# A scan stage on one core: the time step by one Softplus from PSUM, and another table of places

## The chip, the cores and the metric

The kernel runs on one core of a Trainium2 chip. The metric is device time in microseconds (us), the median of some runs. The engines are TensorE (PE; its weight loads are shown as PEld), VectorE (DVE), ScalarE (ACT), GpSimd (POOL) and SyncE (SP), which issues all DMAs here. PSUM is where PE writes; SBUF is the working memory.

## The reference

Four layers work in turn on 64 images of 128 channels by 28x28 pixels (784): a quantised convolution block, an attention block, a Mamba block over the 784 pixels (a selective scan), and a second Mamba over eight tokens a pixel with a group norm. The change is in the third layer. What it must compute, cut to the part that matters, for 160 inner channels d and 24 states n:

```python
delta = jax.nn.softplus(dt @ W_dt.T + b_dt)          # 160 x 784 an image, rank 8
A = -jnp.exp(A_log)
h = jnp.exp(d_t[..., None] * A) * h + (d_t * u_t)[..., None] * B_t[:, None, :]
y = jnp.einsum('bdn,bn->bd', h, C_t)
```

softplus(x) is log(1 + exp(x)); h runs over time, the 784 pixels.

## The kernel before, in words

The program has three stages one behind another: the convolutions (L132-229), a joint stage for attention and the first Mamba (attention_and_mamba, L614-1198; "the scan stage" here), and the token Mamba (token_mamba, L1200 on).

In the scan stage four kinds of work overlap over the images. attention (L783) computes queries and keys (qt, kt), the row maxima mx on DVE, the exponentials et on ACT from products qt,kt in a PSUM bank, and the sums et,vt on PE. inputs (L899; its places are called "prepare") makes the inner channels u, the gate z, the rows B and C (sent to DRAM as bcd), and the time step; delta and delta times u go to DRAM as dud, ten DMAs an image. The scan itself takes 30 pieces an image, five groups of 32 channels by six groups of four states, each a tile of 128x784: inject on POOL (h = ur * Br), decay on ACT (a = exp(dr * A), into one of two PSUM buffers, L1106), scan on DVE (tensor_tensor_scan), the product with Cr on DVE for 18 of the pieces and on POOL for 12, and sums on PE (y from h by fold). The rows Br, Cr, dr and ur are spread by DMA from bcd and dud. The tiles h have nine buffers (L1094). after (L1019; "end") projects out and writes the inputs of the token stage (tok). All matmuls outside the two kinds with own PSUM tiles (a, y) share three PSUM banks called bank.

The time step before (L970-989): the low-rank product is read from PSUM twice, by Abs and by Relu (six activations), then by softplus(x) = relu(x) + ln(1 + exp(-|x|)) with a correction of the rounding of 1 + e: Exp, Identity and Ln on ACT, one operation on DVE (ab), two on POOL (pos), and a third on POOL for delta times u. The tiles are 128x980 (784 pixels of the first 128 channels, and 196 columns that hold the other 32 in four quarters), from a rotation of three buffers ("both", L778).

Nobody writes the order of this stage by hand. The Python code only records steps in a Plan (L343), and Plan.order (L510) walks a list scheduler: for each engine it takes, among the steps that are ready, the one of lowest rank that can start within a patience; Plan.cost (L477) gives each step an assumed duration and a lag to the steps behind it. Where a plan has a table of places, the rank is 30 times the image plus the number that SCAN_PLACES (L255) has for that step of an image (L516-518). So the table and the assumed durations together decide what stands in each engine's queue; the engines then work through their queues strictly, waiting on semaphores. The token stage has a Plan of its own without a table (it is built with turns False). All instructions of both plans are issued at L595, so that this line stands on nearly every row of the profile, and the tile names tell them apart.

[...]EXP_LN holds Exp and Ln; silus (L892) loads SILU, runs its group and loads EXP_LN again, for u and z and for tok: four loads an image.

Of the kernel before, what the change touches and what calls it, by code (L numbers as in the profile page):

```python
# [19 lines left out]
AF = mybir.ActivationFunctionType  # L20
ALU = mybir.AluOpType
# [206 lines left out]
class Tables:  # L228
# [20 lines left out]
    def use(self, name):  # L249
# [8 lines left out]
        -27.16, 95.44, -15.63, 37.72, -30.51, 57.03, -18.48, -125.52, -178.15, -206.63, -174.65, -197.18,  # L258
        -140.8, -116.57, -149.57, -145.94, -227.75, -111.36, -231.96, -171.87, -173.54, -260.5, -273.42,
        -234.6, -172.96, 10.23, -238.49, -198.04, -9.89, -98.73, -142.5, -119.15, -169.38, -62.95, -220.79,  # L260
        -175.82, -246.73, -295.07, -241.57, -310.14, -274.17, -171.92, -254.19, -311.49, -254.96, -322.3,
        -304.01, -357.57, -440.14, -292.13, -474.41, -320.29, -299.91, -499.4, -397.94, -447.26, -211.4,
        -457.68, -289.19, -314.57, -355.54, -378.5, -341.25, -386.43, -360.43, -490.97, -420.49, -429.83,
        -423.33, -579.73, -530.76, -409.94, -351.63, -324.83, -200.92, -293.69, -397.03, -369.21, -413.66,
        -326.13, -292.8, -382.29, -530.85, -505.9, -426.91, -268.63, -329.47, -406.22, -284.33, -330.23,
        -329.88, -373.65, -354.09, -591.18, -489.62
    ],
    "prepare": [
        -66.92, -102.03, -163.16, -47.03, -103.5, -28.71, -36.86, -46.92, -14.15, -68.57, -96.79, -43.76,
        -9.97, -14.28, -81.51, -17.75, -143.82, -133.62, -89.23, -86.81, -7.36, -92.05, -46.28, 9.23, -0.72,  # L270
        137.5, 74.4, -3.52, -61.63, 47.04, -140.23, -40.33, 37.88, 10.06, -119.58, -6.08, -114.83, -162.58,
        -81.55, -59.2, -187.99, -199.29, -242.26, -6.88, -148.55, -80.7, -52.51, -83.71, -227.33, -125.92,
        -134.66, -35.74, -156.84, -76.92, -60.72, -100.66, -90.48, -87.39, -83.33, -44.33, -184.83, 8.93,
        -122.37, -16.94, -91.6
    ],
    "inject": [
        18.78, -13.04, 39.46, -108.54, -24.16, 8.2, -12.14, 22.57, 73.89, 71.93, 173.68, 188.48, -7.76,
        96.37, 16.03, 77.21, -45.69, -70.69, 26.78, -37.73, -20.28, -51.28, -20.21, 54.87, 95.56, 97.76,
        -73.06, -111.22, -26.41, -52.72, 125.48, -13.26, -27.35, -58.59, -101.61, -144.4, -4.61, -60.31,
        -88.83, 44.3, -73.66, -55.93, -17.9, -28.45, 42.86, -19.08, -6.71, 0.59, -15.68, 33.03, 26.73, 45.2,  # L280
        -30.02, 43.3, 45.01, 18.88, -5.35, -59.09, -62.2, 3.56, 101.99, 59.89, 50.57, -4.07, -66.46, -33.11,
        -59.04, 56.76, -3.76, 49.95, 46.4, 54.58, 78.09, 56.87, 67.69, 78.94, -16.92, 92.45, 162.12, 67.42,
        -27.26, 43.68, -79.78, -22.7, -178.74, -193.89, -149.11, -173.08, -205.47, -217.02, -101.34, -62.16,
        -7.27, -69.71, -80.65, -168.87, -112.09, -96.03, -258.82, -264.84, -190.08, -122.2, -37.5, -160.28,
        23.29, -40.81, -224.12, -94.95, -66.49, -46.3, -106.86, -75.8, -168.43, -150.66, -26.28, 43.69,
        29.69, -93.59, -101.58, -130.67, -248.79, -133.16, -121.54, -20.97, 35.67, 78.52, 38.63, 70.37,
        82.72, 64.67, -88.86, 29.57, -136.68, 57.59, 7.34, 51.64, -33.33, -104.67
    ],
    "decay": [
        -95.2, -84.44, 139.88, -72.09, -197.03, -36.24, -233.95, 27.53, -70.69, -167.37, -8.97, -131.49,  # L290
        -187.81, -41.37, -86.9, 81.55, -95.01, -242.01, -137.6, -103.85, 116.96, -45.81, -149.11, 40.01,
        65.22, -238.07, -222.67, -41.3, -194.35, -87.31, -260.63, -357.86, 64.48, -220.63, -92.14, -142.66,
        -227.46, -230.49, -195.52, -43.46, -50.78, -15.66, 97.53, -76.33, -111.14, -66.31, 126.12, -4.68,
        29.52, -62.6
    ],
    "scan": [
        64.34, -28.04, -128.29, -88.87, 8.4, -73.1, -3.81, -119.89, -103.54, -114.09, -143.02, -108.94,
        -123.94, -52.99, 129.22, -33.73, 7.38, -59.29, -13.77, -60.97, -181.27, -149.78, -51.55, -55.41,
        -167.42, -266.57, -193.49, -252.04, -122.23, -122.66, -227.09, -92.14, 17.3, -138.99, 5.77, -111.11,
        21.49, -54.75, 140.71, 131.97, 13.77, 6.4, 106.63, -36.26, 10.14, 26.05, 97.46, -26.99, 10.86,  # L300
        -39.78, 63.49, 46.08, 57.9, 41.38, 345.66, 22.26, 49, 94.12, 97.27, -13.26, 88.75, 17.09, -19.63,
        94.73, 147.37, 156.04, 329.27, 79.09, 214.57, 175.56, 123.17, 186.44, 269.79, 249.84, 269.7, 53.44,
        156.54, 11.49, 162.67, 94.54, 92.9, 155.53, 72.47, 66.49
    ],
    "sums": [
        -77.34, -87.75, 6.78, -83.9, -97.13, -138.22, -160.32, -250.84, -177.94, -161.76, -138.4, -245.14,
        -194.82, 68.91, -143.78, -66.16, 16.51, 196.24, -93.37, 233.98, 61.03, 123.4, -10.51, -82.35,
        -139.71, -113.24, -305.16, 238.99, 148.82, 156.94, 279.52, 285.83, 102.28, 101.96, 205.62, 21.76,
        159.55, -38.75, 93.99, -8.89
    ],  # L310
    "end": [
        -152.26, 121.85, 137.04, -40.17, 6.91, 58.09, 7.41, 9.83, -12.72, -154.91, -73.79, 48.34, 5.15,
        6.87, 62.19, -39.12, 29.45, 111.87, 36.96, 15.95, -37.92, 52.34, 70.47, 85.33, 225.7, 147.56,
        -22.61, 43.42, -72.62, 156.66, 47.12, 80.71, 39.11, 91.98, 14.61, 113.76, 79.23, -51.66, 20.25,
        7.12, 127.77, 164.81
# [14 lines left out]
class Step:  # L330


    def __init__(self, engine, at, leading):
        self.engine, self.at, self.leading = engine, at, leading
        self.calls, self.tiles, self.after, self.before = [], [], set(), []
        self.us, self.lag, self.shared = 0.0, 0.07, False


class Plan:
# [95 lines left out]
    def add(self, calls):  # L435
# [9 lines left out]
        for engine, method, args, kw in calls:  # L445
            assert engine == step.engine
            named = list(enumerate(args)) + list(kw.items())
            aps = [(k, a) for k, a in named if hasattr(a, "tensor")]
            outs = [a for k, a in aps if k == 0 or k in self.OUT]
            ins = [a for k, a in aps if not (k == 0 or k in self.OUT)]  # L450
            if method == "matmul" and not kw["start"]:
                reads += [self.span(a)[:3] + (0, 1 << 20) for a in outs]
            writes += map(self.span, outs)
            reads += map(self.span, ins)
            us, shared, lag = self.cost(engine, method, outs, ins, args, kw)
            step.us += us
            step.shared |= shared
            step.lag = lag
        for accesses, wrote in ((reads, False), (writes, True)):
# [17 lines left out]
    def cost(self, engine, method, outs, ins, args, kw):  # L477

# [31 lines left out]
    def order(self, lead, patience):  # L510
# [23 lines left out]
        port = 0.0  # L534
# [19 lines left out]
        while True:  # L554
# [13 lines left out]
            clock[s.engine] = end = at + s.us  # L568
# [10 lines left out]
            for o in s.before:  # L579
                o.ready = max(o.ready, end + (0.0 if o.engine == s.engine and s.engine != "sync" else s.lag))  # L580
                o.open -= 1
                if not o.open:
                    insort(ready[o.engine], o, key=lambda s: s.rank)
# [27 lines left out]
SILU = "silu_and_others"  # L611


def attention_and_mamba(tc, tables, x, c2d, s2, b2x15, x2d, utd, ztd, pk3, pk4, vec, v, ident, eps):  # L614
# [11 lines left out]
    with ExitStack() as ctx:  # L626
# [272 lines left out]
        def inputs(x1):  # L899
# [70 lines left out]
            ab, pos = both("ab"), both("pos")  # L970
            for h in range(2):
                acc = bank()[:, :HT]
                product(acc, [(w("WdtT", 0, C, 8), dt[:, HALF[h]])])
                act(ab[:, h, :HT], acc, AF.Abs, bias=v("bdtA"))
                act(pos[:, h, :HT], acc, AF.Relu, bias=v("bdtA"))
            acc = bank()[:, :QT]
            quarters(acc, [(w("WdtT", C, 160, 8), dt)])
            act(ab[:, :, HT:], eighths(acc), AF.Abs, bias=v("bdtB"))
            act(pos[:, :, HT:], eighths(acc), AF.Relu, bias=v("bdtB"))
            yield  # L980
            act(ab, ab, AF.Exp, scale=-1.0)
            w1 = both("w1")
            act(w1, ab, AF.Identity, bias=1.0)
            plan.vector.scalar_tensor_tensor(ab, w1, 1.0, ab, ALU.subtract, ALU.subtract)
            act(w1, w1, AF.Ln)
            yield
            plan.gpsimd.tensor_tensor(pos, pos, ab, ALU.subtract)
            plan.gpsimd.tensor_tensor(pos, w1, pos, ALU.add)
            plan.gpsimd.tensor_tensor(ab, pos, u, ALU.mult)
            dud = rows_dram.tile([2, 160, T], F32, name="dud")  # L990
            for m, src in enumerate((pos, ab)):
# [640 lines left out]
```

## Time and profile before

| what | value |
|---|---|
| median of 3 runs | 13,503.77 us (13,500.2 to 13,507.47) |
| profiled execution: time, span | 13,484.76 us, 13,482.6 us |
| busy over the span: PE, DVE, ACT, POOL | 10,764.5, 11,302.1, 10,309.6, 10,700.2 us |
| table loads on ACT | 262, of 1283 ns, 336.1 us |
| mean granted clock of TensorE | 0.841 |

In the rows of the profile, a group of instructions is given as line, engine, operation, output<-inputs, shape and count, then its busy time and the mean of one in ns, then the idle time of the engine just before them and whom it waited for. The waits view gives "engine tile line <- engine tile: us in total, times, longest". The timeline has the start in us, the duration in us, then the instruction, and in brackets the idle time before it. A busy time is a union: neighbours on one engine overlap a little, so that the sum of single durations is larger.

### The profile page before, as it was taken

Reading aid. Unit: us, or ns where it says so; the run is one execution under the profiler, and the core shown is the slowest. Engines: PE = TensorE matmul, PEld = TensorE weight load, DVE = VectorE, ACT = ScalarE, POOL = GpSimd, SP = SyncE. Lnnn points to the kernel's source line nnn. Section 1 sums busy time; section 2 is a strip of 40 time slices with the busy share of each in tenths; the row PEclk is TensorE's granted clock in tenths of the full one; section 3 lists DMA queues with packets and bytes.
Section 4 is the critical chain, followed back from the end, with each engine's and each line's share of the span. In section 5 each row is a group of like instructions: output and inputs, shape, how many; then the busy total and the mean of one; then the engine's idle time right before and its main releaser. Section 6 shows DMA issues by size and latency. Waiting matters only on the chain. (4 is left out here: it accounts for less than half of the span.)

```text
span 13482.6 us, 196851 instructions
## 1 busy us (share of the span) xinstructions
PE 10764.5 (80%) x66976; PEld 6721.6 (50%) x66976; DVE 11302.1 (84%) x10312; ACT 10309.6 (76%) x24308; POOL 10700.2 (79%) x5432
## 2 busy tenths in 40 slices
PE   9988888888888888888886677777777777777776
PEld 9644344344434434433433556565555655556554
DVE  3558888888888888888887899999999899999988
ACT  2357777777777777777776888888888888888886
POOL 0048888888888888888887888888888888888887
PEclk9978888888888888888887888888888888888887
DMA  3525544544544554454444111121111111111111
GB/s 130 191 83 144 148 138 143 150 134 141 146 142 136 143 151 134 141 153 137 133 142 132 40 50 58 46 59 45 53 53 48 56 51 54 49 57 51 48 54 44
DMA packets 758799, 1350.57 MB, mean 100 GB/s; under 512 B 212768, under 2 KB 396448, under 8 KB 757792
## 3 DMA queue, kind: packets, MB, share of 16 engines
q1 hardware_dynamic: 757792, 1337.99, 33.9%
q8 instruction: 529, 8.67, 0.3%
q14 instruction: 478, 3.92, 0.1%
HBM read 980.75 MB, written 356.65 MB: 99 GB/s over the span
## 5 line engine op out<-in xcount | busy, mean ns | idle before, releaser
L595 ACT ACTIVATE a<-delta,A 128x98 f32<-128x98 f32 x14336 | 3906.2, 365 | 773.0 <-PE y L595 438.2
L595 POOL TENSOR_TENSOR h<-ur,Br 128x784 f32<-128x784 f32 x1920 | 3566.3, 1885 | 262.5 <-PE y L595 170.0
L595 POOL TENSOR_TENSOR db<-u,BC 128x896 f32<-128x896 f32 x1568 | 3257.0, 2101 | 153.0 <-DVE h L595 145.8
L595 PE MATMUL y<-a,ident 128*128 128x280 f32 x7168 | 2059.7, 452 | 735.3 <-DVE a L595 724.1
L595 DVE TENSOR_TENSOR_SCAN a<-a,h 128x784 f32<-128x784 f32 x1152 | 2048.4, 1783 | 306.5 <-ACT a L595 304.8
L595 ACT ACTIVATE a<-dr,A 128x784 f32<-128x784 f32 x1920 | 1731.6, 914 | 602.8 <-DVE h L595 576.5
L595 PEld LDWEIGHTS y<-a,ident 128*128 128x128 f32 x7168 | 1556.6, 220 | 1241.2 <-issue 416.2
L595 POOL TENSOR_TENSOR h<-h,Cr 128x784 f32<-128x784 f32 x768 | 1431.9, 1872 | 607.2 <-DVE h L595 495.5
L595 DVE TENSOR_TENSOR_SCAN h<-a,h 128x784 f32<-128x784 f32 x768 | 1367.3, 1780 | 260.3 <-ACT a L595 249.8
L595 DVE TENSOR_TENSOR h<-h,a 128x896 f32<-128x896 f32 x1344 | 1476.4, 1098 | 42.5
L595 PE MATMUL y<-h,fold 128*32 128x196 f32 x15360 | 1033.0, 382 | 459.5 <-POOL h L595 362.6
L595 DVE TENSOR_TENSOR h<-h,db 128x896 f32<-128x896 f32 x1120 | 1230.6, 1099 | 87.8 <-POOL db L595 1.9
L595 DVE TENSOR_TENSOR h<-a,Cr 128x784 f32<-128x784 f32 x1152 | 1109.9, 968 | 192.3 <-DMA Cr<-bcd 150.7
L595 PEld LDWEIGHTS y<-h,fold 128*32 128x32 f32 x15360 | 427.3, 119 | 1166.6 <-POOL h L595 554.0
L595 DVE TENSOR_TENSOR a<-h,BC 128x896 f32<-128x896 f32 x896 | 976.7, 1090 | 28.4
L595 PE MATMUL bank<-et,vt 112*128 112x392 f32 x1792 | 963.8, 667 | 1.5 <-ACT et L595 1.4
L595 PEld LDWEIGHTS y<-late,ident 128*128 128x128 f32 x7168 | 834.5, 192 | 19.8 <-issue 0.5
L595 PE MATMUL y<-late,ident 128*128 128x112 f32 x7168 | 834.0, 274 | 0.0
L595 ACT ACTIVATE et<-bank 112x392 f32<-112x392 f32 x896 | 406.3, 490 | 479.7 <-PE bank L595 470.4
L595 POOL TENSOR_TENSOR xn<-s,sq 128x784 f32<-128x784 f32 x64 | 118.7, 1854 | 741.4 <-DVE mx L595 734.3
L595 POOL TENSOR_TENSOR a<-a,db 128x896 f32<-128x896 f32 x224 | 517.3, 2309 | 232.6 <-issue 168.7
L595 PE MATMUL bank<-qt,kt 17*112 17x392 f32 x1792 | 671.5, 704 | 16.2 <-ACT et L595 6.2
(223 smaller groups left out, 19738.1 us busy)
## 6 DMA issues: line engine op xcount, KB each, us to landing
Br<-bcd SPq DMA_DIRECT2D x1536, 98.0 KB
Cr<-bcd SPq DMA_DIRECT2D x1536, 98.0 KB
dr<-dud SPq DMA_DIRECT2D x1280, 98.0 KB
ur<-dud SPq DMA_DIRECT2D x1280, 98.0 KB
utd<-tok SPq DMA_DIRECT2D x128, 392.0 KB
ztd<-tok SPq DMA_DIRECT2D x128, 392.0 KB
rows<-utd SPq DMA_DIRECT2D x192, 256.0 KB
xt<-in_x SPq DMA_DIRECT2D x32, 784.0 KB
```

Of the source, the lines that this page charges most:

```text
L595: last = getattr(getattr(nc, engine), method)(*args, **kw)
```

## The change

The time step now comes from ScalarE's Softplus, read once from PSUM. Two banks are filled, each with half of the 784 pixels (392 columns) of 128 channels, and 98 columns that hold the other 32 channels; the last 32 channels take eight matmuls of 98 columns where they took four of 196. ACT loads the table set SOFTPLUS, runs four activations (392 and 98 elements, twice), and loads EXP_LN again; the planner keeps these six instructions together. DVE's operation and two of POOL's are gone, and delta times u stays. Two buffers of "both" are used an image in place of three.

```diff
-            ab, pos = both("ab"), both("pos")
-            for h in range(2):
-                acc = bank()[:, :HT]
-                product(acc, [(w("WdtT", 0, C, 8), dt[:, HALF[h]])])
-                act(ab[:, h, :HT], acc, AF.Abs, bias=v("bdtA"))
-                act(pos[:, h, :HT], acc, AF.Relu, bias=v("bdtA"))
-            acc = bank()[:, :QT]
-            quarters(acc, [(w("WdtT", C, 160, 8), dt)])
-            act(ab[:, :, HT:], eighths(acc), AF.Abs, bias=v("bdtB"))
-            act(pos[:, :, HT:], eighths(acc), AF.Relu, bias=v("bdtB"))
-            yield
-            act(ab, ab, AF.Exp, scale=-1.0)
-            w1 = both("w1")
-            act(w1, ab, AF.Identity, bias=1.0)
-            plan.vector.scalar_tensor_tensor(ab, w1, 1.0, ab, ALU.subtract, ALU.subtract)
-            act(w1, w1, AF.Ln)
-            yield
-            plan.gpsimd.tensor_tensor(pos, pos, ab, ALU.subtract)
-            plan.gpsimd.tensor_tensor(pos, w1, pos, ALU.add)
-            plan.gpsimd.tensor_tensor(ab, pos, u, ALU.mult)
+            delta, du = both("delta"), both("du")
+            accs = [bank()[:, :HW2] for h in range(2)]
+            for h, acc in enumerate(accs):
+                with plan.claiming(delta, *accs), plan.together():
+                    plan.tensor.matmul(
+                        acc[:, :HT], lhsT=w("WdtT", 0, C, 8), rhs=dt[:, HALF[h]], start=True, stop=False,
+                        skip_group_check=True,
+                    )
+                    for j in range(4):
+                        at = j * QT + h * ET
+                        plan.tensor.matmul(
+                            acc[32 * j : 32 * j + 32, HT:], lhsT=w("WdtT", C, 160, 8), rhs=dt[:, at : at + ET],
+                            start=False, stop=True, skip_group_check=True,
+                        )
+            with plan.together():
+                plan.scalar.preload_act_table_set(SOFTPLUS)
+                for h, acc in enumerate(accs):
+                    act(delta[:, h, :HT], acc[:, :HT], AF.Softplus, bias=v("bdtA"))
+                    act(delta[:, h, HT:], acc[:, HT:], AF.Softplus, bias=v("bdtB"))
+                plan.scalar.preload_act_table_set(EXP_LN)
+            yield
+            plan.gpsimd.tensor_tensor(du, delta, u, ALU.mult)
```

All of SCAN_PLACES is replaced by other numbers, and Plan.cost has other assumed durations for the scan stage (the old function stays as rough, and the token stage keeps it):

```diff
     def cost(self, engine, method, outs, ins, args, kw):
+        if not self.turns:
+            return self.rough(engine, method, outs, ins, args, kw)
...
+        if engine == "sync":
+            return 0.45, False, 4.5
+        if engine == "tensor":
+            us = max(0.115, n / 1030) * 2
+            if outs[0].partition_size() == 32:
+                return us / 4 if us > 0.22 else n / 1030 / 2, False, 0.1
+            if ins[0].partition_size() in (16, 17):
+                return us / 2, False, 0.1
+            return us, False, 0.1
+        if engine == "gpsimd":
+            return 0.16 + 0.0021 * n, True, 0.14
...
+        if method == "tensor_tensor_scan":
+            return 0.05 + 0.00209 * n, two, 0.14
```

The old function had, among others, a lag of 2.4 us for a DMA (now 4.5), 0.07 us between engines (now 0.1 or 0.14), and 0.2 + 0.00205 n or more for a scan. Plan.order now also counts 0.17 us on PE where the kind of matmul changes or PE has idled, and 0.12 us from a step to a dependent step on the same engine. The three kinds of matmul are those of 32 output partitions, those of 16 or 17 input partitions, and the others. None of this adds an instruction; it only moves them.

## What is forecast, before the change was run

> **What bounds the kernel now.** I read the busy tenths of the page first: of 40 slices of 337 us, the scan stage, which the change touches, fills some 19, from about 750 to 7300 us.
>
> ```profile
> PE   9988888888888888888886677777777777777776
> DVE  3558888888888888888887899999999899999988
> ACT  2357777777777777777776888888888888888886
> POOL 0048888888888888888887888888888888888887
> PEclk9978888888888888888887888888888888888887
> ```
>
> In that stage PE, DVE and POOL all show 8 and ACT shows 7: no engine is saturated. The busy time of a steady stretch says it exactly.
>
> ```profile
> 2000.00:7000.00 5000.00, 4334.50 (x32335) 2001.71 (x32335) 4206.00 (x3813) 3739.50 (x5564) 4198.85 (x2248) 0.85 0.49 142
> ```
>
> The columns are PE, PEld, DVE, ACT, POOL, clock, DMA share, GB/s. The stretch holds 1,465 decays (row a<-dr below), 30 to an image, so 48.83 images: **102.4 us an image**, of which DVE is busy 86.1, POOL 86.0, ACT 76.6 and PE 88.8. PE's number isn't its need: the clock of 0.85 mixes full and half speed, and the matmul ends are modelled. Every engine idles 13 us or more an image, so the waits are next.
>
> ```profile
> ACT a L595 <- DVE h L595: 411.0, 369, 7.1
> POOL h L595 <- DVE h L595: 394.9, 121, 7.5
> ACT et L595 <- PE bank L595: 360.6, 183, 3.2
> DVE a L595 <- ACT a L595: 228.9, 111, 5.3
> DVE h L595 <- ACT a L595: 210.7, 103, 4.6
> DVE yo L595 <- PE y L595: 147.7, 50, 4.8
> DVE h L595 <- DMA Cr<-bcd: 118.5, 61, 3.8
> ```
>
> DVE's 16.3 idle us an image are 9.0 (439.6/48.83) waiting for a decay of ACT, 3.0 for yo's sums, 2.4 for C rows and 1.9 of small things. POOL in turn waits 8.1 for DVE's scans. One image of the timeline tells why ACT is late.
>
> ```profile
> 4036.91 2.98 PE L595 MATMUL bank<-et,vt 112*128 112x392 f32 x4
> 4037.01 0.88 ACT L595 ACTIVATE et<-bank 112x392 f32<-112x392 f32 x2 [3.16 <-PE bank L595]
> ...
> 4041.50 0.50 ACT L595 ACTIVATE et<-bank 112x392 f32<-112x392 f32 x1 [2.70 <-PE bank L595]
> 4041.89 0.91 ACT L595 ACTIVATE a<-dr,A 128x784 f32<-128x784 f32 x1
> ...
> 4042.91 1.80 DVE L595 TENSOR_TENSOR_SCAN a<-a,h 128x784 f32<-128x784 f32 x1 [5.12 <-ACT a L595]
> ```
>
> PE's queue has the sums et,vt between the score products qt,kt (the next of these start at 4039.82 and take 1.64 us). ACT sits on its next exp until PE has passed both, the decay stands behind that exp, and the scan behind the decay stands still 5.12 us. These are waits made by the order of the queues, and the table of places sets that order.
>
> **The change, part by part.** *Instructions.* Per image, by the rows of the steady stretch.
>
> ```profile
> L595 ACT ACTIVATE a<-dr,A 128x784 f32<-128x784 f32 x1465 | 1320.9, 914 | 429.2 <-DVE h L595 411.0 <-DMA utd<-tok 5.4 <-DMA Cr<-bcd 0.3
> L595 ACT ACT_TABLE_LOAD x196 | 251.5, 1283 | 3.5
> L595 POOL TENSOR_TENSOR pos<-w,pos 128x980 f32<-128x980 f32 x48 | 108.8, 2266 | 63.9 <-ACT w L595 63.9
> L595 POOL TENSOR_TENSOR pos<-pos,ab 128x980 f32<-128x980 f32 x48 | 108.2, 2253 | 75.7 <-DVE ab L595 75.7
> L595 DVE SCALAR_TENSOR_TENSOR ab<-w,ab 128x980 f32<-128x980 f32 x48 | 78.2, 1629 | 14.4 <-ACT w L595 14.4
> ```
>
> POOL loses two of its three 128x980 operations, 2.266 + 2.253 = 4.5 us, and the 2.9 us that it idles ahead of them (139.6/48). DVE loses 1.6 us. ACT loses three Abs and three Relu from PSUM (2 x 584 + 444 and 2 x 580 + 429 ns = 3.2 us) and Exp, Identity and Ln of 128x980 (1.029 + 2 x 1.022 = 3.1 us): 6.3 us. It gains two table loads, 2 x 1.283 = 2.6 us, and four Softplus. The trace has no Softplus; the nearest rows are activations from PSUM with a bias operand, 584 ns at 392 elements and about 340 at 98 (rq at 98 without a bias takes 246, and kt over vt shows some 0.09 for the bias). That makes 2 x 584 + 2 x 340 = 1.85 us. ACT's net is 6.3 - 2.6 - 1.85 = -1.85 us. Were Softplus as dear as two activations the gain would be nil; it can't be below the plain one by more than the bias, so I take the row. The built program holds 128 more loads than before, two an image: the group of Softplus stays whole.
>
> A rule speaks against this edit. The Trainium skill ("ScalarE: Activation LUTs", "What ACT_TABLE_LOAD costs") puts a switch at 1283 ns plus a drain of about 1380, some 2.66 us. This trace shows the 1283, but 3.5 us of idle time ahead of 196 loads in all. By the rule two switches take 5.3 us, ACT is 0.9 us worse off than before, and the burst described below grows by 2.8 us, 0.18 ms over 64 images. By the row the drain is absent. I take the row.
>
> PE trades six matmuls for ten of nearly the same columns (before 2 x 392 and 4 x 196, after 2 x 392 and 8 x 98): bounded by -0.4 and +0.5 us, and covered by PE's 13 idle us. They now take two of the three banks at once and hold them until the last Softplus: what is queued behind on PE (the qk scores and their DVE maxima) has one bank for that long, some 4 us; the cover is again PE's idle time, and without it one bank's round, about 2 us, would come on top. The ten DMAs of dud stay, as does SP's count of about 116 issues an image at 0.43 us, some 50 of 102 us. The du product now stands 17 POOL places ahead of the first inject that needs it, where it stood 26; 17 places are over 30 us, so the two DMA hops between stay covered.
>
> *The order.* All five queues of the stage are rearranged, the token stage isn't (its order is the same, since it keeps the old durations). Three things in the built queues matter.
>
> First, for the first half of an image PE now issues all seven qt,kt before any et,vt, so the wait that cost 5.12 us above should be gone for that half; the second half still interleaves. I count the order's present lateness of ACT as 9.0 us, keep 4 of it.
>
> Second, loads are planned with 4.5 us to landing in place of 2.4, so the C-row wait of 2.4 us should shrink; with yo's and the small ones, I keep 4 of 7.3.
>
> Third, and this costs: ACT's queue has longer bursts with no decay in them. The decays have two PSUM buffers, so when a burst begins DVE has at most two scans, with what stands between, before it starves. Before, the longest burst is 6.4 us (tok's silus), against 7.5 us of DVE work, and no burst forces a stall. After, one burst (four r copies 2.74, two s 2.50, two loads 2.57, Softplus 1.85) is 9.66 us, and one (three z, loads, u, z, five exps, x1) 8.73. Sums of single rows overstate by the overlap of neighbours (ACT 81.9 against 76.5 busy, DVE 90.8 against 86.1), so 9.0 and 8.15; with the next decay's 0.91 they stand against 5.2 and 7.0 us of DVE work. Forced stalls: 4.7 + 2.0 = 6.7 us an image. The third burst, 7.3 us at tok's silus, is covered by 10.4 us of DVE work.
>
> *The sum.* DVE's work is 86.1 - 1.6 = 84.5 (POOL's 81.5, ACT's 74.7). Forced 6.7, left of the late decays 4, minus the share that the forced stalls hide of the other waits: 4 in place of 7.3, less about 2.5. That is 84.5 + 6.7 + 4 + 4 - 2.5 = 96.7 us an image, 5.7 less. Over 64 images: 365 us. The profiled execution's 13,484.8 (span 13,482.6) becomes 13,120; the median of the runs shown, 13,503.8, is 19 above the profiled one, and 13,503.8 - 365 = **13,139**. What is late next is ACT: DVE starves in its two bursts.
>
> **The rivals.** *A, near the floor.* All that the order could cure is cured and only the forced stalls and a little remain: 84.5 + 6.7 + 1.5 = 92.7, 9.7 us an image, 12,883. For it: DVE, POOL and ACT are all under 85. Against: PE's clock, half for 30% of the stretch,[...] no table knows it. Chance 0.15.
>
> *B, only the removed work counts.* The idle time stays 16.3 us: 84.5 + 16.3 = 100.8, 1.6 x 64 = 102 us, 13,400. With POOL as the engine that matters, 4.5 + 2.9 us would come off and B would look like the forecast. Chance 0.10 for times from 13,330 to 13,477.
>
> *C, slower: the bursts starve DVE.* If DVE has caught up with ACT when each burst begins, it loses the burst plus the next decay less the DVE work from one scan to the next. Summed over the 30 gaps between decays of an image, with the rows' durations as above, this is 21.3 us after and 14.5 before. Before, 9.0 of 14.5 was lost in fact, 62%. After, 62% of the way from 6.7 to 21.3 is 15.8, and with the other waits unchanged 84.5 + 15.8 + 7.3 = 107.6, 13,840. It decides from 10.6 us of ACT-made stall an image (102.4 - 84.5 - 7.3). For it: the count. Against: most of the 9.0 was the PE wait above, which isn't a burst. Chance 0.13.
>
> *D, no gain.* Bursts and better order cancel, 13,477 to 13,531. Chance 0.04.
>
> **How the numbers follow.** The forecast has 0.58 (12,960 to 13,330), A 0.15, B 0.10, D 0.04, C 0.13. Within 0.2%, 27 us, a measurement of this kernel can't tell a change from none. Faster by more: 0.58 + 0.15 + 0.10 = 0.83; same 0.04; slower 0.13. The range reaches from below A's centre, 12,820, to 13,560, which leaves out most of C and the floor of A.
>
> **What would show each step.** Steady scan stretch: decays per 5,000 us near 1,551 (30 x 5000/96.7); ACT_TABLE_LOAD still 1283 with next to no idle ahead, x128 more in all; Softplus rows near 584 and 340; the et wait for PE roughly halved from 7.4 us an image; DVE's wait for a decay near 9 to 11 us, most of it in two places behind the Softplus and the u,z silus. If those two places show over 8 us each, C holds. If the token stage (from 7,300 us on, some 6,180 long) changes its length, the sum is wrong in a part that I left untouched. A different share of half clock in the scan stage would make the order's gain more or less than I count.

## The result, and the profile after

| | before | after |
|---|---|---|
| median | 13,501.99 us (13,461.27 to 13,507.47, 4 runs) | 13,261.67 us (13,238.11 to 13,293.56, 4 runs) |
| profiled execution: time, span | 13,484.76, 13,482.6 us | 13,260.31, 13,258.5 us |
| mean granted clock of TensorE | 0.841 | 0.863 |

The ratio is 0.983 (95% interval 0.9802 to 0.9858): 240 us faster, where 365 were forecast (13,139), and inside the range. All of it lies in the scan stage. From the first decay to the last the profiled executions took 6,519 us before and 6,284 after, 235 less; from the last decay to the end they took 6,132 and 6,138.

The busy time of the same steady stretch as before (PE, PEld, DVE, ACT, POOL, clock, DMA share, GB/s):

```profile
2000.00:7000.00 5000.00, 4367.95 (x33868) 2123.63 (x33867) 4361.66 (x3886) 3813.36 (x5608) 4124.37 (x2236) 0.90 0.50 147
```

It holds 1,523 decays, 50.77 images: **98.5 us an image** against 102.4.

```profile
L634 ACT ACTIVATE a<-dr,A 128x784 f32<-128x784 f32 x1523 | 1386.1, 917 | 407.4 <-DVE h L634 393.3 <-DMA Cr<-bcd 0.7 <-DMA raw<-c2d 0.3
```

DVE is busy for 85.9 of them (86.1 before; 84.5 forecast) and idle for 12.6 (16.3 before; 12.2 forecast). POOL has 81.2 and ACT 75.1. So the gain of 3.9 us an image is almost wholly idle time of DVE, and 3.9 x 64 = 250 us is the gain in time. The waits of that stretch tell which:

```profile
POOL h L634 <- PE y L634: 438.6, 106, 6.4
...
ACT et L634 <- PE bank L634: 199.7, 232, 3.1
...
DVE h L634 <- POOL h L634: 181.1, 78, 3.6
...
DVE a L634 <- ACT a L634: 135.6, 143, 3.3
DVE x L634 <- PE bank L634: 132.9, 52, 3.0
...
DVE yo L634 <- PE y L634: 52.6, 45, 3.0
...
DVE h L634 <- ACT a L634: 36.5, 78, 2.5
DVE h L634 <- DMA Cr<-bcd: 33.3, 35, 2.3
```

Per image: DVE's wait for a decay fell from 9.0 to 3.4 us ((135.6 + 36.5)/50.77), yo's from 3.0 to 1.0, the one for C rows from 2.4 to 0.7; ACT's wait for a bank at et fell from 7.4 to 3.9. Two waits of DVE are new: 3.6 us for an inject of POOL, and 2.6 us (0.4 before) for the bank of x, the output of the layer. Both stand behind one burst of ACT, in the timeline of one image:

```profile
4041.10 7.27 POOL L634 TENSOR_TENSOR h<-ur,Br 128x784 f32<-128x784 f32 x4 [6.01 <-PE y L634]
...
4042.83 2.52 ACT L634 ACTIVATE s<-x 32x784 f32<-32x784 f32 x2
4042.99 1.79 DVE L634 TENSOR_TENSOR_SCAN h<-a,h 128x784 f32<-128x784 f32 x1 [3.55 <-POOL h L634]
...
4045.36 0.88 ACT L634 ACTIVATE r<-bank 32x392 f32<-32x392 f32 x1
4046.26 1.28 ACT L634 ACT_TABLE_LOAD   x1
4046.30 0.93 PE L634 MATMUL bank<-r,pk 128*128 128x392 f32 x2 [2.35 <-ACT r L634]
4047.26 0.63 DVE L634 SCALAR_TENSOR_TENSOR x<-bank,vec,x1r 128x392 f32<-128x392 f32 x1 [2.23 <-PE bank L634]
```

POOL's inject waits 6.01 us for PE's sums to free a tile h; the scan that needs it stands still for 3.55 us; then the last copy r stands on ACT behind two copies s (2.52 us), PE's r,pk waits for it, and DVE's x for PE. The table loads come behind that, so DVE's two long stops in this burst end before the loads could matter. Last, the rows of the instructions, the two of VectorE before (L595) and after (L634):

```profile
L634 ACT ACT_TABLE_LOAD x306 | 392.6, 1283 | 5.4
L634 ACT ACTIVATE delta<-bank,vec 128x392 f32<-128x392 f32 x102 | 60.1, 590 | 0.7
L634 ACT ACTIVATE delta<-bank,vec 128x98 f32<-128x98 f32 x102 | 35.1, 344 | 0.0
L595 DVE TENSOR_SCALAR raw<-raw 128x784 f32<-128x784 f32 x48 | 47.9, 998 | 0.0
L595 DVE TENSOR_SCALAR x<-raw 128x784 f32<-128x784 f32 x49 | 76.1, 1553 | 0.0
L634 DVE TENSOR_SCALAR raw<-raw 128x784 f32<-128x784 f32 x49 | 104.9, 2140 | 0.0
L634 DVE TENSOR_SCALAR x<-raw 128x784 f32<-128x784 f32 x49 | 123.0, 2510 | 0.0
```

The Softplus costs nearly what the plain row said (584 and 340 forecast), the loads are 1283 ns with next to no idle time ahead of them (5.4 us at 306) or ahead of the Softplus behind them (0.7 us). The surprise is in the last rows: the clamp of an image's input (raw to raw) took 998 ns before and takes 2,140, and x from raw went from 1,553 to 2,510. Nobody edited them.

### The profile page after: what moved, and what is told of

It reads as the page before. It is cut to its first block, busy times and chain, and to the rows that moved or that the text cites. A ratio compares the mean times of both kernels' runs of the same rounds, so it can differ in the third digit from the quotient of the medians.

```text
span 13258.5 us, 197428 instructions
## 1 busy us (share of the span) xinstructions
PE 10620.6 (80%) x67488; PEld 6777.2 (51%) x67488; DVE 11282.8 (85%) x10248; ACT 10235.6 (77%) x24116; POOL 10388.1 (78%) x5304
## 5 line engine op out<-in xcount | busy, mean ns | idle before, releaser
L634 ACT ACTIVATE a<-delta,A 128x98 f32<-128x98 f32 x14336 | 3906.1, 365 | 784.1 <-PE y L634 475.6
L634 POOL TENSOR_TENSOR h<-ur,Br 128x784 f32<-128x784 f32 x1920 | 3536.8, 1870 | 827.7 <-PE y L634 543.0
L634 POOL TENSOR_TENSOR db<-u,BC 128x896 f32<-128x896 f32 x1568 | 3256.2, 2100 | 151.0 <-DVE h L634 143.5
L634 PE MATMUL y<-a,ident 128*128 128x280 f32 x7168 | 2054.1, 451 | 738.8 <-DVE a L634 715.0
L634 DVE TENSOR_TENSOR_SCAN a<-a,h 128x784 f32<-128x784 f32 x1152 | 2052.0, 1785 | 193.4 <-ACT a L634 177.1
L634 PEld LDWEIGHTS y<-a,ident 128*128 128x128 f32 x7168 | 1553.2, 220 | 1243.5 <-issue 436.9
L634 ACT ACTIVATE a<-dr,A 128x784 f32<-128x784 f32 x1920 | 1747.1, 917 | 546.1 <-DVE h L634 526.8
L634 POOL TENSOR_TENSOR h<-h,Cr 128x784 f32<-128x784 f32 x768 | 1433.9, 1875 | 211.0 <-DVE h L634 203.9
L634 DVE TENSOR_TENSOR_SCAN h<-a,h 128x784 f32<-128x784 f32 x768 | 1366.8, 1780 | 266.7 <-POOL h L634 221.6
L634 DVE TENSOR_TENSOR h<-h,a 128x896 f32<-128x896 f32 x1344 | 1476.4, 1099 | 42.5
L634 DVE TENSOR_TENSOR h<-h,db 128x896 f32<-128x896 f32 x1120 | 1230.7, 1099 | 90.4 <-POOL db L634 3.8
L634 DVE TENSOR_TENSOR h<-a,Cr 128x784 f32<-128x784 f32 x1152 | 1106.0, 966 | 60.9 <-DMA Cr<-bcd 38.3
L634 PE MATMUL y<-h,fold 128*32 128x196 f32 x15360 | 990.5, 366 | 74.3 <-POOL h L634 58.2
L634 DVE TENSOR_TENSOR a<-h,BC 128x896 f32<-128x896 f32 x896 | 976.9, 1090 | 28.4
L634 PEld LDWEIGHTS y<-late,ident 128*128 128x128 f32 x7168 | 834.5, 192 | 19.8 <-issue 0.5
L634 PE MATMUL y<-late,ident 128*128 128x112 f32 x7168 | 834.0, 274 | 0.0
L634 PE MATMUL bank<-et,vt 112*128 112x392 f32 x1792 | 812.2, 596 | 19.9 <-ACT et L634 14.4
L634 PE MATMUL bank<-qt,kt 17*112 17x392 f32 x1792 | 702.7, 639 | 136.0 <-ACT et L634 91.9
L634 PEld LDWEIGHTS y<-h,fold 128*32 128x32 f32 x15360 | 443.1, 117 | 624.4 <-issue 285.0
L634 POOL TENSOR_TENSOR xn<-s,sq 128x784 f32<-128x784 f32 x64 | 118.9, 1858 | 764.2 <-ACT sq L634 753.2
L634 POOL TENSOR_TENSOR a<-a,db 128x896 f32<-128x896 f32 x224 | 516.0, 2303 | 230.5 <-issue 162.7
L634 DVE TENSOR_TENSOR h<-a,db 128x896 f32<-128x896 f32 x224 | 475.6, 2123 | 202.0 <-POOL a L634 194.5
```

The costliest lines, as they stand in the source:

```text
L634: last = getattr(getattr(nc, engine), method)(*args, **kw)
```

## The experiments

Three theories stood at the start or came up on the way. T1 is the forecast's: DVE stops where ACT works through a burst without a decay, so the bursts' length, loads included, sets what is left. T2: what DVE misses in the burst is not a decay but sums and copies that stand late in PE's and ACT's queues, so one of them moved or one more buffer gives time back. T3: DVE's own work is the bound, and part of it is the wait of its tensor_scalars for GpSimd, which sits inside their durations. Beside them stands rival B, only the removed work counts.

Times are compared by the ratio to the kernel before, measured beside each run; per image is 150,000 us over the decays in 5,000 us. Medians of different runs are compared only roughly: beside them, the median of the kernel before lay between 13,478 and 13,502 us. "Input" is the mean of the two tensor_scalars of an image's input together. DVE's idle time is the rest of the image. The waits for a decay are those that the list of waits names so; with twice the loads, r before s and both of these, another 2.0 to 2.1 us belong to them, as is shown below.

| run | median us | ratio (95%) | us an image | DVE busy | DVE waits for a decay | input |
|---|---|---|---|---|---|---|
| before | 13,502 | 1 | 102.4 | 86.1 | 9.0 | 2.6 |
| after | 13,262 | 0.983 (0.9802-0.9858) | 98.5 | 85.9 | 3.4 | 4.7 |
| Softplus, old order | 13,509 | 1.001 (0.9999-1.0021) | 102.0 | 83.9 | 11.5 | 2.1 |
| et,vt between qt,kt | 13,774 | 1.0207 (1.0182-1.0231) | 107.8 | 86.4 | 12.5 | 5.0 |
| no loads | 13,304 | 0.9857 (0.9827-0.9886) | 99.3 | 87.1 | 2.9 | 5.6 |
| twice the loads | 13,540 | 1.0032 (1.0021-1.0042) | 103.1 | 87.3 | 3.8 | 5.7 |
| ten tiles h | 13,444 | 0.9965 (0.9952-0.9977) | 101.5 | 88.2 | 2.7 | 6.5 |
| r before s | 13,370 | 0.9918 (0.9903-0.9932) | 101.0 | 87.1 | 3.7 | 5.5 |
| both of these | 13,378 | 0.9915 (0.9898-0.9932) | 101.0 | 85.3 | 4.5 | 3.6 |
| du three times | 13,885 | 1.0282 (1.0253-1.0311) | 109.0 | 91.1 | 2.9 | 8.8 |
| two injects twice | 13,322 | 0.9871 (0.9859-0.9884) | 99.7 | 87.2 | 3.1 | 5.7 |
| no clamp | 13,192 | 0.9774 (0.9756-0.9792) | 97.5 | 85.5 | 3.7 | 4.1 |
| three operands | 13,370 | 0.9905 (0.9889-0.992) | 100.2 | 87.9 | 2.9 | 6.5 |
| other shape | 13,206 | 0.98 (0.9786-0.9813) | 97.3 | 83.4 | 3.5 | 1.9 |

### The removed work, and the order

**Softplus in the old order.** The kernel before, with its table and its assumed durations, but with Softplus in place of the long formula, Identity in place of Abs; the removed operations leave gaps in the queues, nothing else moves. In short, and with the second Relu, Identity and Ln left out of the print:

```diff
-                act(pos[:, h, :HT], acc, AF.Relu, bias=v("bdtA"))
...
-            act(ab, ab, AF.Exp, scale=-1.0)
+            preload_act_table_set(SOFTPLUS); act(pos, ab, AF.Softplus); preload_act_table_set(EXP_LN)
...
-            plan.vector.scalar_tensor_tensor(ab, w1, 1.0, ab, ALU.subtract, ALU.subtract)
...
-            plan.gpsimd.tensor_tensor(pos, pos, ab, ALU.subtract)
-            plan.gpsimd.tensor_tensor(pos, w1, pos, ALU.add)
```

> Softplus alone, in the queues of before: DVE's ab operation, both pos operations of GpSimd, three Relu, Identity and Ln are taken out of the queues, Abs becomes Identity, and at Exp's place stand load, one Softplus of 128x980, load; everything else keeps its place. Per image that removes 1.6 us of DVE, 4.5 of GpSimd and about 1.1 of ScalarE. If the gain comes from the order of the queues (my theory), the old waits on et and yo stay and this saves 0 to 1.6 us an image: 13,400 to 13,500. If the gain comes from the removed work (rival), it is near the changed kernel: 13,230 to 13,300.

No gain that can be measured: 1.001. DVE does 2.2 us an image less and is idle 1.9 more. The waits of this run show where they went:

```profile
ACT et L595 <- PE bank L595: 351.6, 230, 3.6
DVE a L595 <- ACT a L595: 325.1, 145, 5.3
DVE h L595 <- ACT a L595: 236.9, 100, 4.6
```

DVE's wait for a decay rose from 439.6 to 562.0 us in the stretch while et's wait stayed at 352. In the old order the work of DVE and POOL was not what set the time; ACT behind PE was. Rival B falls.

**et,vt between qt,kt.** The changed kernel with one part of the new order undone, on PE's queue alone: in the first half of an image's attention four of the seven et,vt go back between the qt,kt.

```diff
...
+            for m in image.values():
+                for product, steps in ((2, m["vt"][:2]), (3, m["vt"][2:4])):
+                    for s in steps:
+                        order.remove(s)
+                    at = order.index(m["kt"][product])
+                    order[at:at] = steps
```

> The changed kernel with one part of its new order undone: in the first half of an image's attention, four of TensorE's seven et,vt products are issued again between the qt,kt products (two before the third pair, two before the last), as they were in the kernel before; the queues of the other engines are kept. The forecast's step on TensorE's order (ScalarE waits for a bank behind et,vt, the decays come late, VectorE's scan idles) credited 4 of 9.0 us an image: undone, ScalarE's wait for a bank at et goes from 3.9 back towards 7.4 us an image, VectorE's wait for a decay rises by about 4, and the time by 4 x 64 = 256 us, to about 13,520. Rival: ScalarE runs far enough ahead in the new order that the wait is covered: et's wait grows, VectorE's wait for a decay by less than 0.5 us, and the time stays within 13,260 to 13,300.

It took 13,774 us, some 510 more than the changed kernel and twice what the forecast's step gave. Three waits of the run, then one image of its timeline:

```profile
ACT et L648 <- PE bank L648: 626.0, 245, 4.0
DVE a L648 <- ACT a L648: 540.9, 187, 8.7
DVE h L648 <- ACT a L648: 39.9, 142, 0.9
```

```profile
4068.70 2.98 PE L648 MATMUL bank<-et,vt 112*128 112x392 f32 x4
4068.84 0.50 ACT L648 ACTIVATE et<-bank 112x392 f32<-112x392 f32 x1 [4.03 <-PE bank L648]
...
4073.29 0.89 ACT L648 ACTIVATE et<-bank 112x392 f32<-112x392 f32 x2 [3.95 <-PE bank L648]
4074.07 1.76 ACT L648 ACTIVATE a<-dr,A 128x784 f32<-128x784 f32 x2
...
4075.09 1.80 DVE L648 TENSOR_TENSOR_SCAN a<-a,h 128x784 f32<-128x784 f32 x1 [8.39 <-ACT a L648]
```

It is the picture of the kernel before, worse: et waits for PE's et,vt and qt,kt, the decay stands behind et, the scan behind the decay, now for 8.39 us where it was 5.12. Per image et's wait went from 3.9 to 13.5 us and DVE's wait for a decay from 3.4 to 12.5; the image grew by 9.3. Four products moved in one queue thus cost more than the whole change gains. The copy isn't the old order (et waits longer than the 7.4 us of before, and TensorE's clock in the stage is 0.82, with 0.85 before), so the 510 us are not this step's share of the 240. The new order with the long formula wasn't run: how much the shorter time step adds within the new order isn't shown.

### The burst

**No loads.** Left out: the two loads, and softplus itself (Exp in its place, which the resident set has). Queues and places as in the changed kernel.

```diff
-                plan.scalar.preload_act_table_set(SOFTPLUS)
...
-                    act(delta[:, h, :HT], acc[:, :HT], AF.Softplus, bias=v("bdtA"))
+                    act(delta[:, h, :HT], acc[:, :HT], AF.Exp, bias=v("bdtA"))
...
-                plan.scalar.preload_act_table_set(EXP_LN)
```

> The changed kernel without the two table loads around the time step, and with Exp in place of Softplus (so the time step is exp(x), not softplus(x)); all queues otherwise the same. The burst of ScalarE gets 2.57 us shorter. Theory 1 (the forecast: DVE starves for decays behind the burst) expects all of it back, 2.57 x 64 = 164: about 13,100. Theory 2 (the two long stalls there are for GpSimd's inject behind late sums and for the bank of r,pk behind the r copies, which stand ahead of the loads) expects 0.3 to 0.9 us an image: 13,200 to 13,245.

**Twice the loads.** Two more loads in the same group.

```diff
-                plan.scalar.preload_act_table_set(SOFTPLUS)
+                for name in (SOFTPLUS, EXP_LN, SOFTPLUS):
+                    plan.scalar.preload_act_table_set(name)
```

> The changed kernel with four table loads around the time step in place of two, all queues otherwise the same: the burst gets 2.57 us longer. Theory 1 expects +164: about 13,425. Theory 2 expects less, because the decay behind the burst is late by under 1 us now and has to become late first, but then nearly all: +60 to +150, 13,320 to 13,410. No change would say that ScalarE has slack there.

2.6 us less of ACT in the burst gave nothing (0.9857 against 0.983); DVE's two stops there were 3.5 and 2.6 us as before. 2.6 us more cost some 280 us, 4.4 an image. So the loads are just covered: they lie behind the copy that ends DVE's stop, and DVE has work until the next decay, for which it stops 0.35 us in the mean. Lengthened, they come out there: DVE stops for 2.9 us at that scan, and for 1.1 at the second x. The list of waits puts 2.0 of the 2.9 us to POOL's du, but that is a coincidence of times:

```profile
4008.42 2.26 POOL L634 TENSOR_TENSOR du<-delta,u 128x980 f32<-128x980 f32 x1 [3.32 <-PE bank L634]
4009.65 0.92 ACT L634 ACTIVATE a<-dr,A 128x784 f32<-128x784 f32 x1
4010.67 1.80 DVE L634 TENSOR_TENSOR_SCAN a<-a,h 128x784 f32<-128x784 f32 x1 [2.65 <-POOL du L634]
```

The decay ends at 4010.57 and du at 4010.68; both start behind the Softplus. In the run without loads the same scan starts while du still runs, at 3375.48 with du's end at 3375.65, so it doesn't need du:

```profile
3373.32 2.33 POOL L634 TENSOR_TENSOR du<-delta,u 128x980 f32<-128x980 f32 x1
3375.48 1.79 DVE L634 TENSOR_TENSOR_SCAN a<-a,h 128x784 f32<-128x784 f32 x1
```

It is the decay behind the burst that DVE waits for. T1 is right that the burst's length limits DVE, and wrong on what comes first: in the changed kernel DVE stops earlier, for the inject and for x, and the decay is ready soon after.

**Ten tiles h; r before s; both.** The first takes away what POOL's inject waits for (a tile h). The second moves the last copy r on ACT ahead of two copies s.

```diff
-                t = pool.tile(shape, dtype, name=name, tag=tag or name, bufs=bufs)
+                t = pool.tile(shape, dtype, name=name, tag=tag or name, bufs=10 if name == "h" and bufs == 9 else bufs)
```

```diff
...
+            for i, j, k in zip(at, at[1:], at[2:]):
+                if kind(i) == kind(j) == ("prepare", "s") and kind(k) == ("end", "r"):
+                    order[i], order[j], order[k] = order[k], order[i], order[j]
```

> The changed kernel with ten buffers for the tiles h in place of nine, queues unchanged. GpSimd's inject then no longer waits for the late sums at the place where it idles 4.4 us. If the scan's 3.4 us wait for that inject is a wait for a buffer (theory 2), it goes, at most 3.4 x 64 = 218 us, and I expect half, the rest turning into the next wait: 13,050 to 13,180. If something else is late at the same time (the decays, or r,pk), less than 40 us: 13,220 to 13,270.

> The changed kernel with one move in ScalarE's queue: the last r copy stands ahead of the two s copies inside the Softplus burst, not behind them. Theory 2: r,pk and with it VectorE's x2, which waits 2.6 us, come 2.5 us earlier, up to 2.5 x 64 = 160 us: 13,100 to 13,200. Theory 1 (the burst's whole length counts, as the decay stands behind all of it) expects no change: 13,240 to 13,290.

> Both: ten buffers for h and the last r copy ahead of the two s copies. If the two waits (3.4 and 2.6 us, one right behind the other) are separate, the gains add up: 12,950 to 13,120. If the decay behind the burst then becomes what is late (theory 1's floor of 4.7 us for this burst), the sum of both gains is less than 1.3 us an image: 13,180 to 13,262.

Each did what it was made for, and each made the kernel slower. With ten tiles the wait for POOL is gone (3.6 to 0.0 us an image). In its place DVE meets POOL's run of injects with its clamp:

```profile
L634 DVE TENSOR_SCALAR raw<-raw x49: 1521/9374/9482, 2064.6 to 6936.4; 128x784 f32<-128x784 f32 x49
```

(The tile view: shortest, median and longest in ns.) In the median the clamp took 9.4 us, the image's input 6.5 us in the mean, and DVE waited 2.9 us for a second yo and 1.2 more for C rows. With r before s the waits for x fell from 2.6 to 0.8 us, and DVE stops for 3.2 us at the scan behind it (0.35 before). The list puts 2.1 of these to POOL's du; as with twice the loads it is the decay behind the loads. Added up over the burst, DVE's stops are 7.2 us an image in the changed kernel and 7.0, 7.9 and 7.7 in these three: what is taken from one wait comes back at the next. T2 falls as a way to get time: the chains over POOL's inject, over the last r and over the decay end close together, and with r moved T1's decay is what is late. All of it at once (no loads, ten tiles, r ahead) wasn't run. Why these runs end at 101 us, above the 98.5, and not level with it, isn't shown beyond these waits.

### GpSimd beside VectorE

**du three times; two injects twice.** Both give POOL repeated work, about 4.5 and 3.8 us an image; the first in one piece at the product du, the second at two places apart.

```diff
             plan.gpsimd.tensor_tensor(du, delta, u, ALU.mult)
+            plan.steps[-1].calls = plan.steps[-1].calls * 3
```

```diff
...
+                    for j in (back[4], back[14]) if len(back) > 14 else ():
+                        pool[j].calls = pool[j].calls * 2
```

> The changed kernel with the product du computed three times in a row on GpSimd, which gives back the 4.5 us an image that the change took off, at one place, with all queues otherwise the same. If GpSimd has slack (it idles 17 us an image), the time rises by less than 60 us: 13,260 to 13,320. If GpSimd's work is what paces the new order (rival), it rises by about 4.5 x 64 = 290: 13,550.

> The changed kernel with two of an image's inject products computed twice, 4 and 14 injects ahead of du: 3.8 us of GpSimd's work given back as in the run with du three times (4.5 us, +620), but spread. If that run was slow because the 6.8 us stood in one piece ([...]7.7 us in place of 0.56), this one costs much less, under 120 us: 13,262 to 13,380. If any GpSimd work counts more than its own time in this order (rival), it costs 3.8/4.5 of 620, about 520: 13,700 to 13,800.

One piece cost 623 us, 9.7 an image, twice its own length; spread, nearly the same work cost 60 us, 0.9 an image. A timeline of the first shows the larger half of the difference:

```profile
4085.18 3.66 POOL L634 TENSOR_TENSOR h<-h,Cr 128x784 f32<-128x784 f32 x2
4087.98 6.69 DVE L634 TENSOR_SCALAR raw<-raw 128x784 f32<-128x784 f32 x1
4088.79 5.46 POOL L634 TENSOR_TENSOR h<-ur,Br 128x784 f32<-128x784 f32 x3
```

The clamp begins while a product runs on GpSimd, and ends at 4094.67, just behind the three injects that follow it (4094.25). The shortest that this instruction took in the kernel before is 556 ns. It isn't du itself that it waits for: du was over 22 us earlier, and the later queue of GpSimd has moved so that a run of injects without a gap now lies on the clamp. In its mean the clamp, the tensor_scalar on raw, took 7.7 us here; DVE's work grew by 5.2 us an image, and its idle time by as much (yo, mx and C rows). The list of waits shows nothing of the first, since VectorE counts as busy.

**No clamp; three operands; other shape.** Left out in the first: the clamp and rounding of an image's input. The other two compute what the changed kernel does; their diffs show the calls that are issued, at the old places, and leave out the constant columns cc and the helper in_rows (it writes 784 as 7 x 112).

```diff
-            plan.vector.tensor_scalar(raw, raw, 15.0, MAGIC, ALU.min, ALU.add)
-            plan.vector.tensor_scalar(x0, raw, MAGIC, 1.0 / 15.0, ALU.subtract, ALU.mult)
+            plan.vector.scalar_tensor_tensor(raw, raw, 15.0, cc[:, 0:1].broadcast_to([C, T]), ALU.min, ALU.add)
+            plan.vector.scalar_tensor_tensor(x0, raw, MAGIC, cc[:, 1:2].broadcast_to([C, T]), ALU.subtract, ALU.mult)
```

```diff
+        lines7 = wp.tile([C, 7, 113], F32, name="lines7")[:, :, :112]
...
-            plan.vector.tensor_scalar(raw, raw, 15.0, MAGIC, ALU.min, ALU.add)
-            plan.vector.tensor_scalar(x0, raw, MAGIC, 1.0 / 15.0, ALU.subtract, ALU.mult)
+            plan.vector.tensor_scalar(lines7, in_rows(raw), 15.0, MAGIC, ALU.min, ALU.add)
+            plan.vector.tensor_scalar(in_rows(x0), lines7, MAGIC, 1.0 / 15.0, ALU.subtract, ALU.mult)
```

> This leaves part of the computation out: the clamp and rounding of an image's input (VectorE's first tensor_scalar, raw to raw), so x0 is not rounded; every queue is otherwise that of the changed kernel. In the changed kernel that instruction took 2,140 ns in the mean (shortest in the kernel before 556 ns), and the next, x from raw, 2,510 ns (shortest 556). T3 (VectorE is the bound, and its tensor_scalars wait out GpSimd): VectorE has 2.1 us an image less, so 2.1 x 64 = 137 us less, about 13,125 us; if the wait for GpSimd's run only moves to the instruction behind it, x from raw grows to 3 to 4 us and the gain is 20 to 60 us. T1 and T2 (ScalarE's bursts set the image's time): nothing, 13,250 to 13,270, and VectorE's 2.1 us come back as idle time in the Softplus burst (places 44 and 46 of the image).

> The same arithmetic as the changed kernel, but the two tensor_scalars (raw to raw, raw to x) are written as scalar_tensor_tensor with a constant column as the third operand; the order of every queue is kept. The nearest row is the changed kernel's scalar_tensor_tensor on raw, 1,026 ns, which no GpSimd work delayed there (1,023 to 1,027), though the same instruction took up to 2,735 ns in the kernel before. T3, if this form does not wait for GpSimd: 2,140 + 2,510 become 2 x 1,030 ns, 2.6 us an image less, 166 us in all, about 13,095 us. If this form waits as the other does: both stay at 2 to 3 us, and the time is 13,260 to 13,300. T1 and T2: the 2.6 us turn into idle time of VectorE in the Softplus burst, 13,240 to 13,270.

> The same arithmetic as the changed kernel in the same order on every engine; the clamp of an image's input is written to a tile of seven rows of 112 with a gap between them, and x is made from that tile, so source and result of each tensor_scalar are cut differently (784 against 7 x 112). T3: in this form the two instructions [...]wait for no GpSimd instruction; the nearest row of that speed is the changed kernel's scalar_tensor_tensor of 784, 1,026 ns, never delayed there. 2,140 + 2,510 become 2 x 1,000 ns or so with hardly any spread, 2.6 us an image less on VectorE, and at the one-to-one rate that the runs with more VectorE work showed (+1.8 us an image gave +109 us) about 2.6 x 64 = 170 us less than the changed kernel: 13,090 us, faster than both kernels. If the form waits as before: both keep 1.5 to 9 us, 13,260 to 13,300. T1 and T2 (ScalarE's bursts, late sums and copies set the image's time): the instructions shorten, VectorE's idle time in the Softplus burst grows by as much, 13,240 to 13,270.

Without the clamp most of the wait moved one instruction on: x from raw took 4,098 ns in the mean, so the input fell only from 4.7 to 4.1 us, and the kernel gained some 70 us. With a third operand from SBUF the two instructions wait just as much and run longer (medians 1,965 and 2,641 ns; 6.5 us in the mean): some 100 us slower than the changed kernel, 1.7 us an image for 1.8 us more work. The third form does not wait:

```profile
L634 DVE TENSOR_SCALAR lines<-raw x49: 955/956/959, 2018.9 to 6697.9; 128x784 f32<-128x784 f32 x49
L634 DVE TENSOR_SCALAR x<-lines x49: 955/957/962, 2034.7 to 6713.2; 128x784 f32<-128x784 f32 x49
```

Beside the same GpSimd work the spread is gone, 955 to 962 ns, at a shortest time that is 400 ns longer. DVE's work fell by 2.5 us an image, to 83.4. The image of the profiled execution fell by 1.2: 1.3 us came back as idle time, nearly all of it in the wait for C rows (0.7 to 1.9). In the times a gain over the changed kernel isn't shown with certainty: the ratio of 0.98 (0.9786-0.9813) overlaps 0.983 (0.9802-0.9858), and of the 55 us between the medians 24 are between those of the kernel before beside them (13,478 and 13,502). T3 is right on the mechanism and, by these profiles, half right on the price: 1.8 us more work of DVE cost 1.7, 2.5 us less gave 1.2 before another wait was late.

The Trainium skill says why the form matters. "SBUF — State Buffer" ("SBUF: two separate sides") calls the second port pair of VectorE a lock that GpSimd shares; VectorE needs it in a two-port mode, or with two inputs from SBUF against a GpSimd instruction that reads SBUF, and the loser blocks. "VectorE: DVE Perf Modes" ("What auto-detection actually checks") has the two-port mode only where source and result have outermost dimensions both even or equal. 784 against 7 rows is neither, and 956 ns in place of 556 agrees with an instruction that has left that mode; the run with three operands, two of them tensors in SBUF, agrees with the other case. The runs go beyond the page in one point: the wait isn't for one GpSimd instruction of 1.87 us but often for all of a run without gaps (9.4 us with ten tiles h, where a product and four injects lie ahead).

## Why the forecast was right, and where it was off

The direction, the stage and the totals held: idle time of DVE 12.6 us an image against 12.2 in the sum, work 85.9 against 84.5. The missing 1.8 us x 64 = 115 us make 13,139 into 13,254. That the idle time comes so near is luck: the sum has 6.7 + 4 us of waits for decays where 3.4 were measured (its own sign was 9 to 11), and lacks 6.2 us of waits for an inject and for x.

*Instructions.* ACT's terms held (Softplus 590 and 344 ns for 584 and 340; 75.1 us of work an image for 74.7). The drain that the Trainium skill adds to a load ("ScalarE: Activation LUTs", "What ACT_TABLE_LOAD costs") isn't in this trace: 5.4 us of idle time ahead of 306 loads, and no gain at all when they are taken out. DVE's term was mis-sized: 1.6 us of work go, but its work fell by 0.2. The tensor_scalars of the input wait 2.1 us an image longer for GpSimd (4.7 in place of 2.6), as the new places put them beside GpSimd's instructions. Plan.order does count with this wait: in its assumed times no such instruction of VectorE overlaps one of GpSimd (its flag shared). The engines don't keep to the assumed times, and the queues alone don't hold the two apart. The scan stage's other rows of that kind nearly cancel: raw from raw, s and idn got 0.8 us shorter (1,844 to 1,026 ns), the two sums of x with rd 0.7 longer (885 to 1,220 ns each); 0.6 us is left over. The rows of the profile before held the sign of this, 998 and 1,553 ns for two instructions of one shape, and the forecast took such rows as fixed.

*The order, first.* Right in mechanism, and the main cause of the gain as far as is shown: the removed work alone gave nothing, and this step undone on PE alone costs 510 us. It was sized with caution: of 9.0 us of late decays 4 were kept beside 6.7 of forced stalls; in fact 3.4 are left of both together.

*Second.* 4 of 7.3 us of other waits were kept; yo, C rows and the small ones come to about 3.0 (12.6 less 3.4, 3.6 and 2.6). Right.

*Third, the step that failed*: "Forced stalls: 4.7 + 2.0 = 6.7 us an image", waits for a decay, "most of it in two places behind the Softplus and the u,z silus". The size is near and the reason is not. Behind the Softplus burst DVE stops for 6.2 us for an inject and for x, and for only 0.35 for the decay. Behind the u,z silus it stops for 0.6 us at the first scan and for 1.9 at the second, and the decay of the second stands behind exps that wait for PE, which is the first step's pattern and not the burst:

```profile
4098.37 0.50 ACT L634 ACTIVATE et<-bank 112x392 f32<-112x392 f32 x1 [1.05 <-PE bank L634]
4099.64 0.89 ACT L634 ACTIVATE et<-bank 112x392 f32<-112x392 f32 x2 [0.77 <-PE bank L634]
4100.41 1.76 ACT L634 ACTIVATE a<-dr,A 128x784 f32<-128x784 f32 x2
4101.43 1.80 DVE L634 TENSOR_TENSOR_SCAN a<-a,h 128x784 f32<-128x784 f32 x1 [2.21 <-ACT a L634]
```

A count of ACT's burst against two scans can't see that PE's sums and ACT's copies stand in the same burst and stop DVE before the decay does. The decay is next in line: with r moved ahead DVE stops for it for 3.2 us. The loads, counted in that burst's 9.66 us, cost nothing while the other two waits stand ahead of them.

*Rivals.* B is refuted by the Softplus in the old order. C's count of the bursts is refuted in the changed kernel, with 3.4 us of decay waits where it needs 10.6; the run with et,vt between qt,kt shows that 12.5 us of them do make the kernel slower than before. A would have needed the burst's 6 us, which three runs did not get; for another order it isn't refuted.

*The clock.* In the stage it went from 0.85 to 0.90, and to 0.82 in the two slowest runs. It follows the gaps or makes them; these runs don't separate the two.

## What to carry to other kernels

Ask of a queue written by a planner what each engine waits for at the head of its queue, and move the few instructions behind it before removing work elsewhere: here removed work alone gave nothing, and four products of PE put back between others cost 4%. A wait that is taken away shows its worth only when the next one is known: one more buffer cost 1.4% here and an earlier copy 0.9%. Check a named releaser against the end times of others: du was named for waits that were for a decay. Look at the spread of a row's durations too: an instruction that takes 0.56 to 9 us has a wait in it that no list of waits shows.

## What the runs showed of the hardware

A tensor_scalar of 128x784 in SBUF took about 556 ns at the shortest and up to 11 us beside GpSimd; with its result in seven rows with gaps it took 956 ns and never waited. The sum of x with rd, two inputs in SBUF, ranged from 566 to 5,985 ns in the changed kernel. The scans (1,754 to 1,799 ns) and the products with Cr (939 to 977 ns), which read the decay or the scan's result from PSUM, showed no such wait beside the same GpSimd work. So in these runs it is the operands' places and shapes, not the operation, that decide whether VectorE waits.
